# Queries as seven products of halves, and the softmax division moved behind the value products with its inverse sums passed through DRAM

## The chip, the cores and the metric

The kernel runs on one core of one Trainium2 chip, in float32 throughout. The time is device microseconds of that core; lower is better. A core has a TensorE (PE, with its weight loads shown as PEld), a VectorE (DVE), a ScalarE (ACT), a GpSimd (POOL) and a SyncE (SP), which here issues every DMA. Each engine takes its instructions in the order in which they were written.

## The reference, cut to what matters

The block is a cross-attention with adaptive layer norms: 16 batches of 1024 query rows, 64 context rows per batch, width 512, 16 heads of 32.

```python
def _ada_ln(x, c, W_ss, b_ss):
    h = (x - mean(x)) / sqrt(var(x) + EPS)
    scale, bias = split(silu(c) @ W_ss + b_ss, 2)
    return (1.0 + scale)[:, None, :] * h + bias[:, None, :]

xq  = _ada_ln(x_q,  t_vec, Wss_q,  bss_q)       # (16, 1024, 512)
xkv = _ada_ln(x_kv, t_vec, Wss_kv, bss_kv)      # (16, 64, 512)
q = xq @ Wq + bq
k, v = xkv @ Wkv + bkv                          # 16 heads of 32
attn = softmax(q @ k^T / sqrt(32))              # over the 64 context rows
out = attn @ v
return x_q + (out @ Wp + bp)
```

## The kernel before, in words

**Tiling.** The 16 x 1024 query rows are 32 blocks of 512 rows, so two blocks belong to one batch (`i // BPB`). The order of all work is written out by hand: instructions go to each engine's queue in the order of the calls, and the tile pools only add the waits. A start-up stage treats blocks 0 to 2 with separate calls, a loop `for i in range(3, NB - 2)` treats the steady state, and a written-out tail ends blocks 30 and 31. One pass of the loop works on several blocks at once: scores and softmax of block i, values and projection of block i-1, the last projection products of block i-2, queries of block i+1, and the layer norm of blocks i+2 and i+3.

**One block.** `q_stats` (VectorE, L251) and `q_scale` (a few tiny ScalarE and GpSimd operations, L265 to L274) make mean and inverse deviation. `hidden` (ScalarE, L302) normalises. `turn` (VectorE 32 x 32 transposes, L439) and `move` (16 DMAs on SP's queue, L452) bring the features onto the partitions in `xt`. The adaptive scale is folded into the weights: `query_weights` (L431) makes a scaled copy of Wq for every batch, and the shift is folded into a bias. `queries(i, o)` makes one 128-column piece of the queries by four matmuls of 128x128 weights on 512 rows (L487), and `queried` adds the bias on ScalarE (L504). `scores(i, z)` makes the logits of one half of the context with 32x32 tiles of TensorE (L515). Each half lies in two PSUM tiles; VectorE takes the maxima of a tile (L526, a reduction with a transpose inside) and ScalarE then copies it to SBUF (L533). `maxima` joins the halves and spreads them over 32 columns by a transpose (L547), `subtract` takes them away on GpSimd (L560), `weights` is the exponential (L566).

**The division.** `sums(i, z)` makes the row sums of each half (L571), `inverse` adds them, takes the reciprocal and spreads it (L547), and `divide` multiplies both halves by it on GpSimd (L591). `mix` then forms the values with 32x32 tiles (L611).

**The projection.** For blocks 2 to 28 it is already a product of halves: the 512 x 512 product is cut into quarters and made of seven products instead of eight (`product(i, n)`, L740, each 4 matmuls of 256 columns), with sums of the weights made once (`weight_sums`), sums of the value rows made per block (`mixed_halves` on ScalarE, `row_sums` on VectorE, L710 to L714, `last_row_sum` on GpSimd, L719), and each product's bank added to the residual on VectorE (`added`, L754). The accumulation runs through two PSUM banks that are never cleared between products. Two of the four quarters of a block's output need a bias, which `biased` writes into the banks ahead of the products. The other blocks use `project` (L638).

**Memory.** PSUM is two tiles of two banks for scores and values (`ps_s`) and four single banks (`ring`, in the loop 0 and 1 for queries and 2 and 3 for the projection). In SBUF the score tiles `s` rotate through four buffers, the query features `xt` and the queries `qt` through two.

A matmul of float32 shows as two records in the trace, so four matmuls are "x8".

## Time and profile before

| what | value |
|---|---|
| median of 3 runs | 1092.11 us (1091.81 to 1092.3) |
| the profiled execution, whole | 1093.58 us |
| its span, first to last instruction | 1091.8 us |
| granted TensorE clock over the span | 0.998 |
| TensorE busy | 1073.8 us (98%) |
| VectorE busy | 872.9 us (80%) |
| GpSimd busy | 673.4 us (62%) |
| ScalarE busy | 602.6 us (55%) |
| DMA, mean share of 16 engines | 41.4% |

In the tables of the profile a row is one group of instructions: line, engine, operation, output and inputs, count, then busy time and mean nanoseconds of one, then the idle time just before them and what ended it. In a timeline a row is a run of equal instructions: start in us, us from the first one's start to the last one's end, engine, line, operation, count. Matmul records overlap each other by a few tenths of a us, so the price of a run of matmuls is best read from start to start. One loop pass without context work takes 30.84 us; of every four passes one transposes a context tile (+0.43 us) and one makes keys and values (+7.2 us).

### The profile page before, as it was taken

To read this page: it belongs to the slowest core of one execution; us is meant where nothing else is said; L and a number is where in the kernel's file an instruction comes from. 1 tells how busy PE (TensorE), PEld (TensorE's weight loads), DVE (VectorE), ACT (ScalarE), POOL (GpSimd) and SP (SyncE) were. 2 spreads that over 40 slices of the span, in tenths; PEclk is the share of its full clock that TensorE was granted. 3 is DMA by queue.
4 is the path that set the end of the run, shared out by engine and by line. 5 is a ranking of instruction groups with operands and counts; after the bars stand their busy time and mean duration, and the time that the engine had idled before them with its cause. 6 is when DMAs were issued, how large, how long until landed. Compare 5 with 4: busy or idle time off the path is not lost.

```text
span 1091.8 us, 20467 instructions
## 1 busy us (share of the span) xinstructions
PE 1073.8 (98%) x8290; PEld 613.2 (56%) x8290; DVE 872.9 (80%) x1105; ACT 602.6 (55%) x895; POOL 673.4 (62%) x356
## 2 busy tenths in 40 slices
PE   6999999999999999999999999999999999999998
PEld 4534365555755557555566556555665555755533
DVE  5689678888698886989868889688887888697893
ACT  3665545656367572666736575465655656356430
POOL 0247786766748765666737766566765666748830
PEclk9999999999999999999999999999999999999999
DMA  9733532444334443444444443353442444333402
GB/s 338 241 110 116 153 116 103 145 152 149 94 111 144 142 145 113 122 127 142 138 141 128 117 140 126 131 155 121 131 143 91 145 156 136 97 111 100 137 30 87
DMA packets 80525, 145.36 MB, mean 133 GB/s; under 512 B 10504, under 2 KB 10656, under 8 KB 80432
## 3 DMA queue, kind: packets, MB, share of 16 engines
q1 hardware_dynamic: 80432, 144.07, 41.4%
q8 instruction: 65, 1.06, 0.4%
q14 instruction: 28, 0.23, 0.1%
HBM read 77.97 MB, written 33.55 MB: 102 GB/s over the span
## 4 chain that ended last, share of the span: by engine, by line
PE 92%; DMA 3%; DVE 3%; POOL 1%; SPq 1%; issue 0%; ACT 0%; DVEq 0%; POOLq 0%
PE pq L487 38%; PE pp L740 31%; PE po L611 6%; PE ps L515 6%; PE pp L638 6%; PE pv L375 2%; PE pk L347 2%; DMA wss_kv<-in_L_xcond_Wss_kv_dram 1%; DMA b_p_sb<-in_L_xcond_bp_dram 1%; POOL s L591 1%; DVE l L571 1%; DMA x<-in_x_dram 1%; SPq L452 0%; DVE vb L547 0%; DVE s L560 0%; DVE m L526 0%
## 5 line engine op out<-in xcount | busy, mean ns | idle before, releaser
L487 PE MATMUL pq<-xt,wq 128*128 128x512 f32 x1024 | 467.4, 600 | 2.2 <-DMA xt<-ht 1.1
L591 POOL TENSOR_TENSOR s<-s,vb 128x2048 f32<-128x2048 f32 x62 | 280.0, 4538 | 189.6 <-DVE vb L547 183.8
L560 POOL TENSOR_TENSOR s<-s,mb 128x2048 f32<-128x2048 f32 x58 | 262.8, 4554 | 136.7 <-DVE mb L547 136.7
L487 PEld LDWEIGHTS pq<-xt,wq 128*128 128x128 f32 x1024 | 188.8, 190 | 245.6 <-issue 240.4
L533 ACT COPY s<-ps 128x1024 f32<-128x1024 f32 x128 | 129.6, 1012 | 192.0 <-DVE m L526 184.5
L754 DVE TENSOR_TENSOR r<-pp,r 128x512 f32<-128x512 f32 x189 | 126.5, 669 | 69.9 <-PE pp L740 67.1
L504 ACT ACTIVATE qt<-pq,bqs 128x512 f32<-128x512 f32 x128 | 87.6, 685 | 153.0 <-PE pq L487 149.3
L526 DVE TRANSPOSE_TENSOR_REDUCE m<-ps 128x32 f32<-128x1024 f32 x128 | 152.2, 1227 | 24.6 <-PE ps L515 24.6
L566 ACT ACTIVATE s<-s 128x2048 f32<-128x2048 f32 x64 | 122.1, 1908 | 69.0 <-POOL s L560 63.7
L571 DVE TRANSPOSE_TENSOR_REDUCE l<-s 128x64 f32<-128x2048 f32 x64 | 146.6, 2301 | 6.5 <-ACT s L566 6.5
L740 PE MATMUL pp<-w_p_sb,ot 128*128 128x256 f32 x648 | 148.7, 379 | 0.0
L740 PEld LDWEIGHTS pp<-w_p_sb,ot 128*128 128x128 f32 x648 | 123.1, 190 | 28.3 <-ACT x L302 6.5
L740 PE MATMUL pp<-WT,ot 128*128 128x256 f32 x432 | 104.9, 386 | 0.0
L740 PE MATMUL pp<-WT,s 128*128 128x256 f32 x432 | 102.8, 381 | 0.0
L740 PEld LDWEIGHTS pp<-WT,s 128*128 128x128 f32 x432 | 81.5, 190 | 32.2 <-issue 20.8
L302 ACT ACTIVATE x<-x,rstdq 128x512 f32<-128x512 f32 x128 | 97.2, 811 | 3.9 <-POOL rstdq L274 2.2
L740 PEld LDWEIGHTS pp<-WT,ot 128*128 128x128 f32 x432 | 79.8, 190 | 32.4 <-DVE r L754 16.8
L251 DVE BATCH_NORM_STATS2 bs<-x 128x6 f32<-128x512 f32 x128 | 84.4, 660 | 3.9 <-DMA x<-in_x_dram 3.9
L439 DVE STREAM_TRANSPOSE ht<-x 128x512 f32<-128x512 f32 x124 | 77.5, 680 | 5.8 <-DMA xt<-ht 3.3
L547 DVE STREAM_TRANSPOSE mb<-m 128x2048 f32<-128x2048 f32 x32 | 74.0, 2311 | 6.7 <-POOL s L591 3.7
L515 PE MATMUL ps<-qt,kt 32*32 32x512 f32 x2048 | 76.1, 600 | 1.4 <-DVE kt L355 0.8
L547 DVE STREAM_TRANSPOSE vb<-v 128x2048 f32<-128x2048 f32 x32 | 74.0, 2311 | 3.0
(111 smaller groups left out, 871.2 us busy)
## 6 DMA issues: line engine op xcount, KB each, us to landing
x<-in_x_dram SPq DMA_DIRECT2D x32, 1024.0 KB, 5.6
r<-in_x_dram SPq DMA_DIRECT2D x32, 1024.0 KB, 5.5
xt<-ht SPq DMA_DIRECT2D x496, 64.0 KB, 2.0
out_dram<-r SPq DMA_DIRECT2D x54, 512.0 KB, 2.8
out_dram<-r SPq DMA_DIRECT2D x20, 256.0 KB, 2.0
wss_q<-in_L_xcond_Wss_q_dram SPq DMA_DIRECT2D x2, 1024.0 KB, 8.9
ctx<-in_ctx_dram SPq DMA_DIRECT2D x8, 256.0 KB, 5.5
wss_kv<-in_L_xcond_Wss_kv_dram SPq DMA_DIRECT2D x2, 1024.0 KB
```

Source lines behind the costliest of these rows:

```text
L302: nc.scalar.activation(dst, src, AF.Identity, bias=rstd[:, 1, j : j + 1], scale=rstd[:, 0, j : j + 1])
L487: nc.tensor.matmul(pq.rearrange("p (g n) -> p g n", g=4), lhsT=wq_tiles[b][:, c, o * P : (o + 1) * P], rhs=xt[:, :, c, :], start=(c == 0), ...
L515: nc.tensor.matmul(pss[r // 2][32 * c : 32 * c + 32, r % 2, :], lhsT=kt[rows, c, z * HK : (z + 1) * HK], rhs=qt[rows, c, :], start=True, s ...
L526: nc.vector.tensor_reduce(m_tiles[i][:, z, 2 * e : 2 * e + 2, :], pss[e].rearrange("p r (j a) -> p r j a", a=32), AX.X, ALU.max, apply_tra ...
L533: nc.scalar.copy(s_sb[:, 2 * e : 2 * e + 2, :], pss[e])
L547: nc.vector.transpose(t, src.unsqueeze(2).to_broadcast([P, HPC * NJ, 32]))
L560: eng.tensor_tensor(s_tiles[i, z], s_tiles[i, z], mb_tiles[i], ALU.subtract)
L566: nc.scalar.activation(p, p, AF.Exp, scale=SCALE)
L571: nc.vector.tensor_reduce(l_tiles[i][:, z], s_tiles[i, z].rearrange("p r (j a) -> p r j a", a=32), AX.X, ALU.add, apply_transpose=True,)
L591: eng.tensor_tensor(s_tiles[i, z], s_tiles[i, z], vb, ALU.mult)
L740: nc.tensor.matmul(acc[k][:, t * HO : (t + 1) * HO], lhsT=rows[:, c, t * P : (t + 1) * P], rhs=cols[:, c, :], start=new and t == 0 and c == 0,
L754: nc.vector.tensor_add(r, acc[k].rearrange("p (t h) -> p t h", t=2), r)
```

## The change

Four things change, in blocks and passes from about 4 to 29; blocks 0 to 3 and 31 keep plain queries, blocks 0 to 2 and the last two keep the old division.

1. **Queries of blocks 5 to 30** are made from halves in the manner of the projection: seven products of 4 matmuls of 256 columns. The scale and the shift are no longer folded into the weights; `scale_features` applies them to the features on ScalarE, `query_weight_sums` forms sums of the weight quarters once, `feature_sums` forms sums of the feature quarters per block on GpSimd. The results leave their two banks by ScalarE (`query_out`), by VectorE (`query_added`), and one copy from bank to bank (`query_seed`).
2. **The division of blocks 3 to 29** follows `mix`. GpSimd adds the two exponential halves (`total`), VectorE makes one row sum (`row_total`) and its reciprocal, one DMA writes the 128 x 64 inverses to DRAM and four DMAs read them back with the heads turned onto other partitions (`inverse_rows`), VectorE spreads them (`spread_rows`) and multiplies them in while it takes the values out of PSUM (`divided`).
3. **The projection's row sums** all go to GpSimd (`row_sums(i, n)`), and the seven products use another arrangement of signs, so that both biases lie in the banks and `residual_rest` is not needed.
4. **The order** of a loop pass is new: products of projection and queries alternate, layer norm runs one block further ahead, the context work is spread over three passes, in `scores(i, 0)` the copies of the two PSUM tiles are crossed, and the loop starts at block 4 behind a written-out pass for block 3. `qt` and the score tiles get fixed single buffers.

The diff, cut to its core:

```diff
+    def scale_features(i, cs=range(NC)):
+        xt, b = xt_tiles[i], i // BPB
+        for c in cs:
+            nc.scalar.activation(
+                xt[:, :, c, :],
+                xt[:, :, c, :],
+                AF.Identity,
+                scale=ss["q"][:, c, b : b + 1],
+                bias=ss["q"][:, NC + c, b : b + 1],
+            )
+    HO, HT, HC = H // 2, TB // 2, NC // 2
+    sums_of = {}
+    def query_half(m, k):
+        return w_q_sb[:, k * HC : (k + 1) * HC, m * HO : (m + 1) * HO]
+    def query_weight_sums():
+        t = qpool.tile([P, 4, HC, HO], F32, tag="wq", name="wq_sums")
+        sums_of["wq"] = t
+        tt = nc.gpsimd.tensor_tensor
+        tt(t[:, 0], query_half(1, 0), query_half(1, 1), ALU.add)
+        tt(t[:, 1], t[:, 0], query_half(0, 0), ALU.subtract)
+        tt(t[:, 2], query_half(0, 0), query_half(1, 0), ALU.subtract)
+        tt(t[:, 3], query_half(0, 1), t[:, 1], ALU.subtract)
+    def feature_half(i, k, n):
+        return xt_tiles[i][:, 2 * n : 2 * n + 2, k * HC : (k + 1) * HC, :]
+    def feature_sums(i):
+        if "xt" not in sums_of:
+            sums_of["xt"] = qpool.tile([P, 4, 2, HC, P], F32, tag="wq", name="xt_sums")
+        t = sums_of["xt"]
+        tt = nc.gpsimd.tensor_tensor
+        b12 = feature_half(i, 0, 1)
+        tt(t[:, 0], feature_half(i, 1, 1), b12, ALU.subtract)
+        tt(b12, b12, feature_half(i, 0, 0), ALU.subtract)
+        tt(t[:, 1], feature_half(i, 1, 1), b12, ALU.subtract)
+        tt(t[:, 2], feature_half(i, 1, 0), t[:, 1], ALU.subtract)
+    qa = {}
+    def query_product(i, n):
+        w, t = sums_of["wq"], sums_of["xt"]
+        a, x = {
+            1: (query_half(0, 0), feature_half(i, 0, 0)),
+            2: (query_half(0, 1), feature_half(i, 1, 0)),
+            3: (w[:, 3], feature_half(i, 1, 1)),
+            4: (query_half(1, 1), t[:, 2]),
+            5: (w[:, 0], feature_half(i, 0, 1)),
+            6: (w[:, 1], t[:, 1]),
+            7: (w[:, 2], t[:, 0]),
+        }[n]
+        k = 0 if n in (1, 6, 5, 3) else 1
+        new = n in (1, 7)
+        if new:
+            qa[k] = bank(f"pq_{i}_{n}", k)
+        for m in range(2):
+            for c in range(HC):
+                nc.tensor.matmul(
+                    qa[k][:, m * HT : (m + 1) * HT].rearrange("p (g n) -> p g n", g=2),
+                    lhsT=a[:, c, m * P : (m + 1) * P],
+                    rhs=x[:, :, c, :],
+                    start=new and m == 0 and c == 0,
+                    stop=c == HC - 1,
+                    skip_group_check=True,
+                )
+    def query_seed(i):
+        qa[1] = bank(f"pq_{i}_2", 1)
+        nc.scalar.copy(qa[1], qa[0])
+    def query_places(i, n, k, m):
+        pq = qa[k][:, m % 2 * HT : (m % 2 + 1) * HT]
+        dst = qt_tiles[i][:, m, :].rearrange("p (t g b) -> p g t b", t=NT, g=4)
+        return (
+            pq.rearrange("p (g t b) -> p g t b", g=2, t=NT),
+            dst[:, 2 * n : 2 * n + 2],
+        )
+    def query_out(i, n):
+        k, m, h = {2: (1, 0, 0), 6: (0, 1, 0), 7: (1, 1, 1), 3: (0, 0, 1)}[n]
+        if n == 2:
+            qt_tiles[i] = qpool.tile([P, NC, TB], F32, tag="qt", name=f"qt_{i}", bufs=1)
+        for o in (2 * m, 2 * m + 1):
+            src, dst = query_places(i, h, k, o)
+            nc.scalar.activation(dst, src, AF.Identity, bias=bq_t[:, o : o + 1])
+    def query_added(i, n):
+        k, h = {5: (0, 1), 4: (1, 0)}[n]
+        for o in (2, 3):
+            src, dst = query_places(i, h, k, o)
+            nc.vector.tensor_tensor(dst, src, dst, ALU.add)
...
-        for e in range(2):
+        for step in (
+            ((maximum, 0), (copied, 1), (maximum, 1), (copied, 0))
+            if crossed
+            else ((maximum, 0), (copied, 0), (maximum, 1), (copied, 1))
+        ):
+            step[0](step[1])
...
+    def total(i):
+        t = big.tile([P, HPC, TB], F32, tag=f"big{(i + 1) % 2 * 2}", name=f"sum_{i}")
+        nc.gpsimd.tensor_tensor(t, s_tiles[i, 0], s_tiles[i, 1], ALU.add)
+        sum_tiles[i] = t
+    def row_total(i):
+        lt_tiles[i] = small.tile([P, HPC, NJ], F32, tag="lt", name=f"lt_{i}")
+        nc.vector.tensor_reduce(
+            lt_tiles[i],
+            sum_tiles.pop(i).rearrange("p r (j a) -> p r j a", a=32),
+            AX.X,
+            ALU.add,
+            apply_transpose=True,
+        )
+    def inverse_rows(i):
+        lt = lt_tiles.pop(i)
+        nc.vector.reciprocal(lt, lt)
+        v = small.tile([P, NC, NJ], F32, tag="vr", name=f"vr_{i}")
+        d = dram.tile([NC, 32, HPC, NJ], F32, tag="lt", name=f"ltd_{i}")
+        nc.sync.dma_start(d.rearrange("c a r j -> (c a) r j"), lt)
+        for r in range(HPC):
+            nc.sync.dma_start(v[32 * r : 32 * r + 32], d[:, :, r, :].rearrange("c a j -> a c j"))
+        vt_rows[i] = v
+    def spread_rows(i):
+        v = vt_rows.pop(i).rearrange("p c j -> p (c j)")
+        t = qpool.tile([P, NC, TB], F32, tag="vb", name=f"vb_{i}", bufs=1)
+        nc.vector.transpose(
+            t.rearrange("p c q -> p (c q)"), v.unsqueeze(2).to_broadcast([P, NC * NJ, 32])
+        )
+        vb_tiles[i] = t
+    def divided(i):
+        vb = vb_tiles.pop(i)
+        ot_tiles[i] = opool.tile([P, NC, TB], F32, tag="ot", name=f"ot_{i}")
+        for e in range(2):
+            cs = slice(2 * e, 2 * e + 2)
+            nc.vector.tensor_tensor(ot_tiles[i][:, cs, :], po_tiles[i][e], vb[:, cs, :], ALU.mult)
...
+    def row_sums(i, n):
+        tt = nc.gpsimd.tensor_tensor
+        if n == 0:
+            s1_tiles[i] = opool.tile([P, HC, HT], F32, tag="s1", name=f"s1_{i}")
+            tt(s1_tiles[i], half_rows(i, 1, 0), half_rows(i, 0, 0), ALU.subtract)
+            tt(half_rows(i, 1, 0), half_rows(i, 1, 1), half_rows(i, 1, 0), ALU.subtract)
+        else:
+            s2_tiles[i] = opool.tile([P, HC, HT], F32, tag="s2", name=f"s2_{i}")
+            tt(s2_tiles[i], half_rows(i, 1, 1), s1_tiles[i], ALU.subtract)
+            tt(half_rows(i, 0, 1), half_rows(i, 0, 1), s2_tiles[i], ALU.subtract)
...
-    residual(2, (0, 1))
     context_features(2)
-    query_weights(2)
+    scale_features(4)
     project(1, 2)
+    load_x(6)
+    scores(3, 0, crossed=True)
+    project(1, 3)
+    ring[:] = [0, 1]
+    scores(3, 1)
+    maxima(3)
+    subtract(3)
+    queries(4, 0)
+    load_residual(3)
+    hidden(5, (0, 1))
+    biased(2, 2)
+    mix(2)
+    mixed(2)
+    hidden(5, (2, 3))
+    q_stats(6)
+    turn(5, range(NT))
+    move(5)
+    q_scale(6)
+    row_sums(2, 0)
+    load_x(7)
+    queries(4, 1)
+    product(2, 1)
+    added(2, 1)
+    product(2, 2)
+    weights(3, 0)
+    added(2, 2)
+    biased(2, 3)
+    weights(3, 1)
+    total(3)
+    queries(4, 2)
+    keys(2)
+    hidden(6, range(NT))
+    scale_features(5)
+    row_sums(2, 1)
+    turn(6, range(NT))
+    load_x(8)
+    product(2, 7)
+    q_stats(7)
+    value_products(2)
+    value_tiles(2)
+    row_total(3)
+    inverse_rows(3)
+    queries(4, 3)
+    feature_sums(5)
+    move(6)
+    q_scale(7)
...
+    for i in range(4, NB - 2):
+        a, b, n, f = i - 1, i - 2, i + 1, i + 2
         kvb = i // 4 * 2 + 2
         kv = i % 4 if kvb < B else None
         if kv == 0:
             load_context(kvb)
+        scores(i, 0, crossed=True)
+        product(b, 6)
+        added(b, 6)
+        query_product(n, 1)
+        query_seed(n)
+        added(b, 7)
         scores(i, 1)
+        product(b, 5)
+        added(b, 5)
         maxima(i)
         subtract(i)
+        product(b, 4)
+        if i + 3 < NB:
+            hidden(i + 3, (0, 1, 2))
+        query_product(n, 2)
+        query_out(n, 2)
+        product(b, 3)
+        spread_rows(a)
+        if i + 3 < NB:
+            hidden(i + 3, (3,))
+        added(b, 4)
+        added(b, 3)
+        biased(a, 2)
         load_residual(i)
+        mix(a)
+        divided(a)
+        row_sums(a, 0)
+        query_product(n, 6)
+        weights(i, 0)
+        query_out(n, 6)
         if kv == 1:
             context_hidden(kvb)
+        scale_features(f, (0, 1))
+        product(a, 1)
+        if i + 4 < NB:
+            q_stats(i + 4, (0,))
+        added(a, 1)
+        product(a, 2)
+        if i + 4 < NB:
+            q_stats(i + 4, (1,))
+        added(a, 2)
+        weights(i, 1)
+        total(i)
+        query_product(n, 7)
+        query_out(n, 7)
+        biased(a, 3)
+        scale_features(f, (2, 3))
+        row_sums(a, 1)
+        if kv == 1:
+            context_scaled(kvb)
+        if kv == 2:
+            key_products(kvb, spare(f"pk_{kvb}"))
+        if kv == 3:
+            value_products(kvb, spare(f"pv_{kvb}"))
+        if i + 3 < NB:
+            turn(i + 3, range(NT))
+        if i + 5 < NB:
+            load_x(i + 5)
+        elif i == NB - 3:
             load_residual(NB - 1)
+        query_product(n, 5)
+        query_added(n, 5)
+        if i + 4 < NB:
+            q_stats(i + 4, (2,))
+        if kv == 1:
+            context_scale(kvb)
+        if kv == 2:
+            key_tiles(kvb)
+        if kv == 3:
+            value_tiles(kvb)
+        query_product(n, 4)
+        query_added(n, 4)
+        if i + 4 < NB:
+            q_stats(i + 4, (3,), kvb=kvb if kv == 0 else None)
+        query_product(n, 3)
+        query_out(n, 3)
+        if f < NB - 1:
+            feature_sums(f)
         else:
             residual(i)
+        product(a, 7)
+        row_total(i)
+        inverse_rows(i)
+        if i + 3 < NB:
+            move(i + 3)
+        if i + 4 < NB:
+            q_scale(i + 4, kvb=kvb if kv == 0 else None)
+        if kv == 1:
+            context_shift(kvb)
...
+    scores(y, 0, crossed=True)
+    product(y - 2, 6)
+    added(y - 2, 6)
+    added(y - 2, 7)
+    scores(y, 1)
+    product(y - 2, 5)
     added(y - 2, 5)
-    scores(y, 0)
-    product(y - 2, 4)
-    added(y - 2, 4)
-    product(y - 2, 3)
-    added(y - 2, 3)
-    ring[:] = [0, 1, 2, 3]
-    load_residual(y)
-    scores(y, 1)
     maxima(y)
     subtract(y, nc.vector)
     queries(z, 0)
+    product(y - 2, 4)
+    product(y - 2, 3)
+    spread_rows(y - 1)
+    added(y - 2, 4)
+    added(y - 2, 3)
+    ring[:] = [1, 2, 3, 0]
+    load_residual(y)
     mix(y - 1)
-    mixed(y - 1)
+    divided(y - 1)
     weights(y, 0)
     queries(z, 1)
     sums(y, 0)
```

## The prediction

> **What bounds the kernel now.** I read the page's busy times and the chain that ended last first.
>
> ```profile
> PE 1073.8 (98%) x8290; PEld 613.2 (56%) x8290; DVE 872.9 (80%) x1105; ACT 602.6 (55%) x895; POOL 673.4 (62%) x356
> ...
> PE 92%; DMA 3%; DVE 3%; POOL 1%; SPq 1%; issue 0%; ACT 0%; DVEq 0%; POOLq 0%
> PE pq L487 38%; PE pp L740 31%; PE po L611 6%; PE ps L515 6%; PE pp L638 6%; PE pv L375 2%; PE pk L347 2%; DMA wss_kv<-in_L_xcond_Wss_kv_dram 1%; DMA b_p_sb<-in_L_xcond_bp_dram 1%; POOL s L591 1%; DVE l L571 1%; DMA x<-in_x_dram 1%; SPq L452 0%; DVE vb L547 0%; DVE s L560 0%; DVE m L526 0%
> ```
>
> TensorE carries 92% of the chain, and the queries (L487) are its largest line. Busy time alone would not prove this, since matmul records overlap, so I took TensorE's timeline of one plain loop pass:
>
> ```profile
> 460.60 1.14 PE L515 MATMUL ps<-qt,kt 32*32 32x512 f32 x32
> 461.67 1.99 PE L740 MATMUL pp<-WT,ot 128*128 128x256 f32 x8
> 463.50 1.89 PE L740 MATMUL pp<-w_p_sb,ot 128*128 128x256 f32 x8
> 465.32 1.14 PE L515 MATMUL ps<-qt,kt 32*32 32x512 f32 x32
> 466.39 3.70 PE L487 MATMUL pq<-xt,wq 128*128 128x512 f32 x8
> 470.02 2.35 PE L611 MATMUL po<-s,vt 32*32 32x512 f32 x64
> 472.30 3.70 PE L487 MATMUL pq<-xt,wq 128*128 128x512 f32 x8
> 475.84 3.62 PE L740 MATMUL pp<-w_p_sb,ot 128*128 128x256 f32 x16
> 479.29 3.60 PE L487 MATMUL pq<-xt,wq 128*128 128x512 f32 x8
> 482.73 1.89 PE L740 MATMUL pp<-WT,s 128*128 128x256 f32 x8
> 484.45 1.89 PE L740 MATMUL pp<-WT,ot 128*128 128x256 f32 x8
> 486.18 3.60 PE L487 MATMUL pq<-xt,wq 128*128 128x512 f32 x8
> 489.61 1.89 PE L740 MATMUL pp<-WT,s 128*128 128x256 f32 x8
> 491.43 1.14 PE L515 MATMUL ps<-qt,kt 32*32 32x512 f32 x32
> ```
>
> Start to start nothing is missing: no wait ends late, the pass is 491.43 - 460.60 = 30.83 us of matmuls. A quarter of the queries costs 3.43 us, a product of halves 1.73; either costs about 0.1 more on each side where a 32x32 stage (L515, L611) is its neighbour.
>
> Then the other engines' prices:
>
> ```profile
> L591 POOL TENSOR_TENSOR s<-s,vb 128x2048 f32<-128x2048 f32 x62 | 280.0, 4538 | 189.6 <-DVE vb L547 183.8
> ...
> L754 DVE TENSOR_TENSOR r<-pp,r 128x512 f32<-128x512 f32 x189 | 126.5, 669 | 69.9 <-PE pp L740 67.1
> ...
> L526 DVE TRANSPOSE_TENSOR_REDUCE m<-ps 128x32 f32<-128x1024 f32 x128 | 152.2, 1227 | 24.6 <-PE ps L515 24.6
> ...
> L571 DVE TRANSPOSE_TENSOR_REDUCE l<-s 128x64 f32<-128x2048 f32 x64 | 146.6, 2301 | 6.5 <-ACT s L566 6.5
> ...
> xt<-ht SPq DMA_DIRECT2D x496, 64.0 KB, 2.0
> ```
>
> Their idle times show that they wait for each other and for TensorE while TensorE waits for no one.
>
> **TensorE's part.** Four quarters with their neighbours cost 3.63 + 3.53 + 3.43 + 3.44 = 14.03 us in this pass. In the new pass stand 14 products, 14 x 1.725 = 24.15, six of them beside a 32x32 stage (+0.6), two score stages of 1.07 and one value stage of 2.28: 29.17 us instead of 30.84. That is 1.67 less, for blocks 5 to 30, so **26 x 1.67 = 43.4 us**. Weight loads grow from 32 to 56 per block at 190 ns; under a 256-column record (214 ns) the same load already hides in the projection rows, by 24 ns. The projection keeps 27 x 7 products, keys and values stay, only spread over three passes.
>
> **The other engines, per pass.** VectorE loses three row sums (0.60 start to start), one of two L571 reductions (2.28) and a small join (0.3), and gains two 128x1024 products out of PSUM (no row; between two L754 at 0.60 and L526 at 1.23 each; I take 1.15, so 2.3) and four 128x256 adds (0.36 from the 256-wide value copies, 1.44): 26.3 becomes 25.7 of 29.2. ScalarE loses 5.2 (four L504, the value copies, the scaled weights) and gains four feature scalings at 0.76, eight 256-wide copies (no row; between 0.31 for 64 columns and 0.60 for 512; 0.43) and the seed 0.5: about 21. GpSimd loses 9.06 + 1.27 + 1.27 and gains 4.53 (`total`) and eight 512-wide sums at 1.25: about 24.3. SP gains five issues at 0.6. All fit under 29.2, hidden behind TensorE; but queues are in order, so I walked one pass, t = 0 at its first score stage.
>
> - Scores 1 at 4.73; its maxima, `added` 5 and `maxima` give the spread maximum at 11.68. Subtractions end at 16.4 and 20.9, the second exponential at 22.8, `query_out` 7 at 23.7. Query product 4 needs that bank and can start at 23.95: **0.2 us of room**.
> - GpSimd: `row_sums` 0 to 23.5, `total` to 28.1; VectorE's `row_total` and reciprocal to 31.1, which is 1.9 in the next pass. Behind them wait the next maxima; their copies end at 4.2, scores 1 wants the banks at 4.73: 0.5 of room. As a loop (subtractions 9.06, row sums 2.5, total 4.53, row total 2.3, reciprocal 0.55, maxima and adds 9.2, handovers 0.5) this is 28.7 against 29.17.
> - SP: write landed at 4.0, reads issued by 6.5, landed at 8.0; `spread_rows` comes at 11.68, **3.7 of room**, and behind it are `added` 4 and 3, `divided` (its first half 0.6 ahead of product 1). The 16 moves queue behind the reads: 10.0 us of issue as now, landed at 18; `scale_features` wants them at 19.2, and behind it on ScalarE stands the second exponential: 1.2 of room.
>
> So nothing overshoots, but the rooms are tenths, and on passes with a context tile ScalarE has 0.76 more ahead of the exponential. The two passes in four that make keys or values have 3.6 us more TensorE work and absorb all of it; that leaves 14 passes. I charge 0.35 each, **4.9 us** (0 if every room holds).
>
> [...] For the two DMA hops the row is 2.0 us from issue to landing for 64 KB in 512-byte pieces. [...] I take the row: DMA is at 41%, and the 1 MB load ahead has landed by then. [...] The trace shows it once in the tail: a GpSimd add of 1.27 us took 2.79 beside a VectorE subtraction of two SBUF tiles. `divided` reads one tile from PSUM, as L754 does, beside which the 58 GpSimd subtractions stay within 4530 to 4581 ns. [...]
>
> **Once only.** The pass for block 3 does two blocks' layer norm: 16 moves end near 157, the next load of x lands near 162.6 (5.6 later), its statistics hold VectorE until 166, then value copies and the row total; the next maxima start about 3.5 us late, the scores' wait costs **3.3** (0 to 9). In the tail no query product stands between products 6 and scores 1 of block 30, which then wait **1.4** for the copies. `query_weight_sums` (4 x 1.26) fits between the end of `queries(1, 3)` at 60.6 and GpSimd's first division at 66.9; uncovered, it would delay that division, which is on the chain.
>
> **Sum.** 1091.8 - 43.4 + 4.9 + 3.3 + 1.4 = 1058.0 us of span; this execution as a whole was 1.8 above its span and 1.5 above the median of the runs, so a median of about **1058**.
>
> **Rivals.**
> - *The helper loop binds* (0.25). The 28.7 us loop over GpSimd and VectorE and ScalarE's bank release have almost no room; 7% on their prices makes the pass 30.7, 14 x 1.5 = 21.5 instead of 4.9: **1075** (1066 to 1086). For it: three of my prices have no row. Against: VectorE and GpSimd durations spread by 1%.
> - *SP's loop binds, and it gets slower* (0.09). Reciprocal, write 2.1, reads 2.4, moves 10, landing 1.4, scaling 1.6, exponential 1.9, total 4.5, row total 2.3, reciprocal and handovers 1.1: 27.3 us. If small transfers land like the worst in the table (7.4 for a move) or issue at 1.6, it grows by 4 to 6. It decides from 31.9 us (14 x 2.76 eats the 38.7 left): 4.6 more than the row. At 6 more, 14 x 4.1 + 12 x 0.6 = 65: **1117**. Against: 496 moves have a median of 2.0 and hardly vary.
> - *Seven products save nothing* (0.03). If a product costs 1.96 because its features come in two runs of 128 columns and the load's 24 ns are lost, four quarters and seven products are equal: about **1093** unless the stalls add more. Against: L487 already reads four such runs.
> - *As forecast* (0.63): 1048 to 1066.
>
> **How the numbers follow.** The runs differ by 0.05%, and about 0.2% (2.2 us) is what can be told from no change. Forecast and first rival are faster: 0.88. The third lies within with 0.02 and slower with 0.01, so slower is 0.10. The range runs from 43.4 saved and no stall (1048) into the first rival at 1080, which leaves out about 0.06 of it, the other two, and a little of the forecast.
>
> **What would show it.** Plain passes of 29.2 to 29.6 us between score stages, products of 1.73 in both groups, TensorE at 98%, small reads landing near 2 us, VectorE never idle for `v` ahead of the spread. Wrong would be: weight loads of query products waiting for ScalarE's `qt`, GpSimd subtractions over 4.6 us, ScalarE's scaling waiting for the moves' landing, or score stages waiting for copies in every plain pass.

## The result, and the profile after

The changed kernel took 1058.55 us (median of 4 runs, 1057.48 to 1060.34) against 1092.2 us for the kernel before (4 runs, 1091.81 to 1093.16). The ratio is 0.9692, with a 95% interval of 0.9675 to 0.9709: 3.1% faster. The profiled execution took 1058.86 us with a span of 1057.1 us, so the span is compared with the 1091.8 us of before: 34.7 us less.

The page of the changed kernel, its busy times, the chain that ended last and the groups that answer to those shown of before:

```profile
PE 1033.6 (98%) x8914; PEld 733.7 (69%) x8914; DVE 854.7 (81%) x1134; ACT 618.0 (58%) x951; POOL 752.7 (71%) x470
...
PE 80%; DVE 5%; POOL 5%; DMA 4%; SPq 2%; issue 2%; ACT 1%; POOLq 0%; DVEq 0%; ACTq 0%
...
L729 POOL TENSOR_TENSOR s<-s,mb 128x2048 f32<-128x2048 f32 x58 | 263.1, 4560 | 160.8 <-DVE mb L716 160.8
...
L655 ACT ACTIVATE qt<-pq,bias_t 128x256 f32<-128x256 f32 x208 | 85.8, 463 | 110.9 <-PE pq L625 110.9
...
L768 POOL TENSOR_TENSOR sum<-s,s 128x2048 f32<-128x2048 f32 x27 | 122.7, 4543 | 0.8 <-ACT s L735 0.8
...
L662 DVE TENSOR_TENSOR qt<-pq,qt 128x256 f32<-128x256 f32 x104 | 39.1, 418 | 63.1 <-PE pq L625 62.5
```

TensorE is still busy for 98% of a shorter span, and it still carries most of the chain. The other engines did not become cheaper as a whole: VectorE falls by 18 us, ScalarE rises by 15 and GpSimd by 79. GpSimd's subtraction, 4560 ns against 4554 before, kept its price. The new loop adds work to the helpers to take work from TensorE.

The timeline of TensorE over one plain pass of the changed kernel (pass 16), start in us and us from the first start to the last end:

```profile
542.48 1.14 PE L673 MATMUL ps<-qt,kt 32*32 32x512 f32 x32
543.55 2.00 PE L933 MATMUL pp<-WT,s 128*128 128x256 f32 x8
545.38 1.89 PE L625 MATMUL pq<-xt,w_q_sb 128*128 128x256 f32 x8
547.20 1.14 PE L673 MATMUL ps<-qt,kt 32*32 32x512 f32 x32
...
562.94 1.89 PE L625 MATMUL pq<-xt_sums,wq_sums 128*128 128x256 f32 x8
564.67 1.89 PE L625 MATMUL pq<-xt,wq_sums 128*128 128x256 f32 x8
...
569.85 1.89 PE L933 MATMUL pp<-WT,ot 128*128 128x256 f32 x8
571.66 0.71 PE L673 MATMUL ps<-qt,kt 32*32 32x512 f32 x16
```

The last row is cut short by the end of the view. From score stage to score stage this pass is 571.66 - 542.48 = 29.18 us. There is no wait in it, and the products of both groups stand 1.73 us apart (564.67 - 562.94). Before, the same pass was 30.83.

The small transfers, in the table of DMA issues of the changed kernel (count, size of each, median us from issue to landing):

```profile
xt<-ht SPq DMA_DIRECT2D x496, 64.0 KB, 2.0
...
vr<-ltd SPq DMA_DIRECT2D x108, 8.0 KB, 1.6
...
ltd<-lt SPq DMA_DIRECT2D x27, 32.0 KB, 1.6
```

**Where the 34.7 us are.** I compared the starts of the first score stage of every pass in the two timelines.

| stretch | after minus before, us | what it is |
|---|---|---|
| up to the scores of block 3 | -1.5 | before had a half-clock window in its start-up (granted clock 0.5 from 78.9 to 82.3 us), after had none there |
| pass 3 | -3.9 | two projection products (3.5) are put off to the tail |
| passes 4 to 29 | -35.6 | 26 x 1.67 = -43.4 (queries of blocks 5 to 30; block 4 still has plain ones), then +5.8 in pass 4 and +2.0 in all others together |
| pass 30 | +4.1 | the two products put off, and a wait of 0.6 |
| scores of block 31 to the end | +2.2 | a slower last softmax |

### The profile page after: what moved, and what is told of

The parts are those of the page before. It is cut to its first block, busy times and chain, and to the rows that moved or that the text cites. A ratio compares the mean times of both kernels' runs of the same rounds, so it can differ in the third digit from the quotient of the medians.

```text
span 1057.1 us, 22537 instructions
## 1 busy us (share of the span) xinstructions
PE 1033.6 (98%) x8914; PEld 733.7 (69%) x8914; DVE 854.7 (81%) x1134; ACT 618.0 (58%) x951; POOL 752.7 (71%) x470
## 3 DMA queue, kind: packets, MB, share of 16 engines
q8 instruction: 70, 1.15, 0.5%
## 4 chain that ended last, share of the span: by engine, by line
PE 80%; DVE 5%; POOL 5%; DMA 4%; SPq 2%; issue 2%; ACT 1%; POOLq 0%; DVEq 0%; ACTq 0%
PE pp L933 28%; PE pq L625 27%; PE po L825 6%; PE ps L673 6%; PE pp L852 5%; PE pq L542 3%; SPq L508 2%; PE pv L431 2%; PE pk L395 2%; POOL s L760 2%; DMA wss_kv<-in_L_xcond_Wss_kv_dram 2%; DMA b_p_sb<-in_L_xcond_bp_dram 1%; POOL s L729 1%; DMA x<-in_x_dram 1%; DVE s L729 1%
## 5 line engine op out<-in xcount | busy, mean ns | idle before, releaser
L729 POOL TENSOR_TENSOR s<-s,mb 128x2048 f32<-128x2048 f32 x58 | 263.1, 4560 | 160.8 <-DVE mb L716 160.8
L685 DVE TRANSPOSE_TENSOR_REDUCE m<-ps 128x32 f32<-128x1024 f32 x128 | 150.6, 1214 | 27.1 <-PE ps L673 27.1
L655 ACT ACTIVATE qt<-pq,bias_t 128x256 f32<-128x256 f32 x208 | 85.8, 463 | 110.9 <-PE pq L625 110.9
L768 POOL TENSOR_TENSOR sum<-s,s 128x2048 f32<-128x2048 f32 x27 | 122.7, 4543 | 0.8 <-ACT s L735 0.8
L933 PEld LDWEIGHTS pp<-WT,s 128*128 128x128 f32 x432 | 78.9, 192 | 54.0 <-issue 29.3
L933 PE MATMUL pp<-WT,s 128*128 128x256 f32 x432 | 109.3, 397 | 0.0
L625 PE MATMUL pq<-xt_sums,wq_sums 128*128 128x256 f32 x416 | 101.0, 386 | 0.0
L321 ACT ACTIVATE x<-x,rstdq 128x512 f32<-128x512 f32 x128 | 96.7, 807 | 4.8 <-POOL rstdq L285 3.2
L625 PE MATMUL pq<-xt,wq_sums 128*128 128x256 f32 x416 | 99.0, 381 | 0.0
L625 PEld LDWEIGHTS pq<-xt_sums,wq_sums 128*128 128x128 f32 x416 | 77.0, 190 | 31.1 <-issue 21.8
L625 PE MATMUL pq<-xt,w_q_sb 128*128 128x256 f32 x416 | 98.4, 380 | 0.1
L662 DVE TENSOR_TENSOR qt<-pq,qt 128x256 f32<-128x256 f32 x104 | 39.1, 418 | 63.1 <-PE pq L625 62.5
L565 ACT ACTIVATE xt<-xt,ss_q 128x512 f32<-128x512 f32 x112 | 84.7, 810 | 6.1 <-DMA xt<-ht 4.3
L625 PEld LDWEIGHTS pq<-xt,w_q_sb 128*128 128x128 f32 x416 | 79.1, 190 | 11.0 <-PE pp L933 0.4
```

The source lines that it names most:

```text
L321: nc.scalar.activation(dst, src, AF.Identity, bias=rstd[:, 1, j : j + 1], scale=rstd[:, 0, j : j + 1])
L565: nc.scalar.activation(xt[:, :, c, :], xt[:, :, c, :], AF.Identity, scale=ss["q"][:, c, b : b + 1], bias=ss["q"][:, NC + c, b : b + 1],)
L625: nc.tensor.matmul(qa[k][:, m * HT : (m + 1) * HT].rearrange("p (g n) -> p g n", g=2), lhsT=a[:, c, m * P : (m + 1) * P], rhs=x[:, :, c, : ...
L655: nc.scalar.activation(dst, src, AF.Identity, bias=bq_t[:, o : o + 1])
L685: nc.vector.tensor_reduce(m_tiles[i][:, z, 2 * e : 2 * e + 2, :], pss[e].rearrange("p r (j a) -> p r j a", a=32), AX.X, ALU.max, apply_tra ...
L729: eng.tensor_tensor(s_tiles[i, z], s_tiles[i, z], mb_tiles[i], ALU.subtract)
```

## The experiments

Passes are given as the time between the first score stages of one block and the next, read from TensorE's timeline. "K" is a pass with keys, "V" one with values, "T" one that turns a context tile (the last of these, pass 29, no longer has a tile to turn). Where one number stands, most passes of that kind have it; pass 4 is left out. The kernel before ran beside each group of kernels, at 1091.9 to 1092.3 us.

| kernel | median us (range) | ratio to before, 95% interval | plain | T | K | V |
|---|---|---|---|---|---|---|
| changed, again | 1057.95 (1056.88 to 1060.41) | 0.9692 [0.9679, 0.9706] | 29.2 | 29.6 | 32.8 | 33.0 |
| four quarters | 1099.08 (1098.1 to 1099.92) | 1.0062 [1.0046, 1.0079] | 30.9 | 31.3 | 34.4 | 34.7 |
| old division | 1143.78 (1142.27 to 1144.26) | 1.0469 [1.0453, 1.0485] | 32.7 | 33.4 | 35.6 | 35.4 |
| the same, deviations first | 1125.75 (1124.34 to 1127.09) | 1.0305 [1.0286, 1.0323] | 31.9 | 32.6 | 34.8 | 34.6 |
| the same, no feature sums | 1144.6 (1142.29 to 1145.86) | 1.0476 [1.0458, 1.0494] | 32.8 | 33.5 | 35.7 | 35.4 |
| no trip | 1057.73 (1056.38 to 1059.44) | 0.9684 [0.967, 0.9699] | 29.2 | 29.6 | 32.8 | 33.0 |
| two more hops | 1102.4 (1097.59 to 1103.16) | 1.0083 [1.0061, 1.0105] | 31.0 to 36.2 | 30.1 to 34.7 | 32.8 | 33.0 |
| moves first | 1117.16 (1109.94 to 1125.33) | 1.0229 [1.0175, 1.0284] | 30.9 to 33.3 | 31.5 to 33.8 | 34.2 to 35.0 | 34.8 to 37.3 |
| one more GpSimd add | 1060.2 (1058.52 to 1061.29) | 0.9704 [0.9688, 0.9721] | 29.2 | 30.0 | 32.8 | 33.0 |
| start reordered | 1055.1 (1054.05 to 1056.24) | 0.9659 [0.9646, 0.9673] | | | | |
| tail reordered | 1056.48 (1055.56 to 1056.81) | 0.967 [0.9657, 0.9684] | | | | |
| both reordered | 1052.36 (1051.78 to 1053.33) | 0.9635 [0.9622, 0.9648] | | | | |

### The changed kernel again

Run beside the three reordered kernels as their yardstick.

> The changed kernel once more, beside the three that follow: 1057 to 1060 us.

It came out at 1057.95 us. Its span is 1055.1 us where the first profile had 1057.1. Half of the difference is pass 4, 34.0 against 35.0 us, where the first execution has a half-clock window, told of below; the other half is small stalls in passes 5 to 29.

### Queries as four quarters

```diff
-        query_product(n, 1)
-        query_seed(n)
+        queries(n, 0, later=True)
...
-        query_product(n, 6)
+        queries(n, 1, later=True)
         weights(i, 0)
-        query_out(n, 6)
+        queried(n, 1)
```

The pieces 2 and 3 are undone in the same way, and `feature_sums` goes. All else, with the new order and the new division, stays.

> The changed kernel with four plain quarters of the queries (512 columns) at the places of query products 1, 6, 7 and 3; the copy from bank to bank, the adds on VectorE and the feature sums on GpSimd (5.1 us a pass) are left out, since nothing needs them. Theory (TensorE's matmuls alone are the gain): a plain pass is 30.82 us of matmuls again, 26 x 1.65 = 43 more, less some 2 us of stalls that disappear: 1098 to 1102 us, no faster than the kernel before. Rival (order, division and GpSimd row sums carry a good part of the gain): clearly under 1085 us.

It took 1099.08 us. The rest of the change without the seven products is 0.6% slower than the kernel before; the seven products alone are worth 1099.08 - 1057.95 = 41.1 us. The passes say the same: four passes in a row take 131.2 us here and 124.7 us in the changed kernel, so one pass gains 1.65 us.

### The old division in the new loop

```diff
-        total(i)
+        sums(i, 0)
...
+        sums(i, 1)
...
-        row_total(i)
-        inverse_rows(i)
+        inverse(i)
+        divide(i)
...
-        divided(a)
+        mixed(a)
```

Beyond these lines, `inverse` now also spreads the sums on VectorE, and `spread_rows` goes.

> The changed kernel with the old division from block 3 on: row sums of both halves on VectorE, inverse and spread, two multiplications on GpSimd ahead of the value products, values copied out by ScalarE; no trip through DRAM. Theory (the division is moved only to make room on GpSimd): GpSimd has 9.06 + 9.06 + 5.1 + 5.1 + 0.8 = 29.1 us of work and about 1 us of handovers in a pass of 29.18, so the 14 passes without keys or values become 30 to 31 us: 1068 to 1085 us, still faster than before. Rival (the division is worth nothing, TensorE alone decides): 1057 to 1061. Rival (the division is most of the gain): over 1085.

This expectation missed by far: 1143.78 us, slower than the kernel before, and every pass is longer, those with keys and values too. Two readings of it were open: GpSimd's load, or the order of the queues. Two more kernels asked for one each. In the first the deviations are made ahead of the division:

```diff
+        if i + 4 < NB:
+            q_scale(i + 4, kvb=kvb if kv == 0 else None)
+        if kv == 1:
+            context_shift(kvb)
         inverse(i)
         divide(i)
```

> The old division in the new loop again (1143.8 us before), with the six small GpSimd operations of the layer norm's deviations (q_scale, and context_shift) emitted ahead of inverse and divide instead of behind them. If the queue order made that kernel slow (hidden and the score copies on ScalarE waiting for deviations that sit behind 9 us of division): 1065 to 1095 us. If GpSimd's own load did (subtraction 9.05, division 9.0, row sums 5.1, feature sums 5.1, small ones 0.8: 29.1 us, and some 3 us of waiting for VectorE's inverse between them): the order changes nothing, 1136 to 1146 us.

In the second the four feature sums are left out of every pass of the loop, 5.1 us of GpSimd, so the query products read the sums of block 5:

```diff
-        if f < NB - 1:
-            feature_sums(f)
-        else:
+        if f >= NB - 1:
             residual(i)
```

> The old division in the new loop again, with the four feature sums (4 x 1.27 us on GpSimd) left out of every pass of the loop, so that query products 4, 6 and 7 read the sums of block 5 (leaves out part of the computation). If GpSimd's load made that kernel slow: its loop falls from about 33 to about 28 us, below TensorE's 29.2, and the time to 1055 to 1080 us. If the order of queues did: 1130 to 1146 us, as with the sums.

Without feature sums the time is 1144.6 us: GpSimd's load is not the cause, against what I had come to think. With the deviations first it is 1125.75 us: this one change of the queue order is worth 18.0 of the 86 us. The wait that this takes away stands in ScalarE's timeline of the first of the three kernels:

```profile
529.05 2.23 ACT L321 ACTIVATE x<-x,rstdq 128x512 f32<-128x512 f32 x3 [3.26 <-POOL rstdq L285]
```

`hidden` (L321) waits 3.26 us for deviations whose four tiny GpSimd operations are queued behind 9.0 us of division, and the value copies wait behind `hidden`. What is left is in the timelines of TensorE and VectorE of the kernel with deviations first, in a plain pass (in it L673 is the scores, L757 the spread of the inverse sums, L685 the maxima, L740 the row reduction of one half):

```profile
577.82 1.26 PE L673 MATMUL ps<-qt,kt 32*32 32x512 f32 x32
...
584.11 1.18 PE L673 MATMUL ps<-qt,kt 32*32 32x512 f32 x32 [1.38 <-ACT s L694]
...
606.06 1.99 PE L625 MATMUL pq<-xt,wq_sums 128*128 128x256 f32 x8 [0.83 <-DVE qt L662]
...
579.57 2.31 DVE L757 STREAM_TRANSPOSE vb<-v 128x2048 f32<-128x2048 f32 x1
581.81 2.34 DVE L685 TRANSPOSE_TENSOR_REDUCE m<-ps 128x32 f32<-128x1024 f32 x2
...
600.70 2.30 DVE L740 TRANSPOSE_TENSOR_REDUCE l<-s 128x64 f32<-128x2048 f32 x1
...
605.29 0.71 DVE L662 TENSOR_TENSOR qt<-pq,qt 128x256 f32<-128x256 f32 x2
```

The 2.31 us spread of the inverse sums stands on VectorE straight ahead of the next maxima, so the second scores come 6.29 us after the first instead of 4.72. One of the two row reductions stands ahead of the addition that frees the bank of a query product. Both are places that the new division leaves free: it has one reduction, and its spread comes later, behind the next maximum. In this kernel TensorE's waits for the score copies add up to 43.1 us and those for the additions to 7.9. A further 9 us lie in pass 4, which lasts 42.7 us instead of 34.0 and holds two half-clock windows; three more stand elsewhere. These causes are read from the trace; no run took them away one by one, and no run has an order made for the old division, so the 86 us are what it costs in this order and not what it must cost.

### The trip through DRAM left out

The five transfers are left out; the spread reads the inverse sums where they lie, with the heads on the wrong partitions, so this leaves out the turn of the inverse sums.

```diff
-        nc.sync.dma_start(d.rearrange("c a r j -> (c a) r j"), lt)
-        for r in range(HPC):
-            nc.sync.dma_start(v[32 * r : 32 * r + 32], d[:, :, r, :].rearrange("c a j -> a c j"))
-        vt_rows[i] = v
+        vt_rows[i] = lt
```

> The changed kernel without the five transfers: the inverse sums are spread from where they lie, so the heads get each other's inverses and the output is not the reference's; nothing else is left out. Theory (the trip is hidden with 4.8 us of room ahead of the spread): no plain pass gets shorter, 1056 to 1060 us. Rival (the trip costs time in every pass): 5 us or more faster than the changed kernel.

1057.73 us: the same as with the trip, and so are the passes. The five transfers cost nothing where they stand.

### Two more hops

```diff
-        nc.sync.dma_start(d.rearrange("c a r j -> (c a) r j"), lt)
+        nc.sync.dma_start(d0.rearrange("c a r j -> (c a) r j"), lt)
+        nc.sync.dma_start(d1, d0)
+        nc.sync.dma_start(d, d1)
```

> The changed kernel with two more transfers of the 32 KB from DRAM to DRAM between the write and the four reads, each waiting for the one before: the trip grows by some 3.7 us. Theory (what stands behind the trip is short of room, not the spread): the inverses still land near 10.2 us into the pass, ahead of the spread at 11.3, but the 16 moves land near 21 instead of 17.4, scale_features wanted them at 18.7, and the second exponential and query product 4 come 1.5 to 2.2 us late in 14 passes: 1078 to 1090 us. Rival (only the spread's wait counts): 1057 to 1061. Rival (the helpers have more room than walked): under 1066.

1102.4 us: 44 us more than the changed kernel, 12 past what I expected at most. The timelines of SP, ScalarE and GpSimd show the chain (this pass makes values), and the rows of waits (us in total, times, longest) what it does in the whole execution:

```profile
535.28 0.49 SPq L791 DMA_DIRECT2D lt<-lt  x1
537.43 0.49 SPq L792 DMA_DIRECT2D ltd<-lt  x1
539.42 1.76 SPq L794 DMA_DIRECT2D vr<-ltd  x4
541.28 11.11 SPq L508 DMA_DIRECT2D xt<-ht  x16
...
553.97 1.52 ACT L565 ACTIVATE xt<-xt,ss_q 128x512 f32<-128x512 f32 x2 [4.53 <-DMA xt<-ht]
555.39 1.90 ACT L735 ACTIVATE s<-s 128x2048 f32<-128x2048 f32 x1
...
557.36 4.53 POOL L768 TENSOR_TENSOR sum<-s,s 128x2048 f32<-128x2048 f32 x1 [3.65 <-ACT s L735]
...
ACT xt L565 <- DMA xt<-ht: 81.6, 27, 4.9
...
PE pq L625 <- ACT qt L655: 26.7, 14, 3.7
```

The four reads are issued 5.4 to 7.5 us after the write, 6.1 on average (here 7.5; the write, not shown, stands at 531.93), where the changed kernel has 1.5 to 3.5 and an average of 2.1. So the trip is 4.0 us longer, about what I expected. The moves (L508) start that much later, `scale_features` (L565) waits for them in every pass, the second exponential stands behind it, and GpSimd's `total` and the copy that frees the bank for query product 4 stand behind that. It is at product 4 that TensorE waits: in all 13 shorter passes and in pass 4, never in those with keys or values. This is the handover for which the prediction had 0.2 us of room. The loop is the one that my slower rival had summed to 27.3 us; with 4.0 us more it is 31.3. The runs agree in both respects: passes of 32.8 and 33.0 are untouched, and of the 13 shorter ones the eight without half clock last 31.1 us on average. The other five last 34.5. They contain six half-clock windows, each up to 1.7 us dear (half of 3.41 us, an estimate), where the changed kernel has none in the loop behind pass 4. Without these the 13 passes would have cost some 13 x 1.65 = 21 us, within what I expected; what I had not reckoned with is that such waits, of 1.92 to 3.75 us in these five passes, were followed by half clock.

### The moves ahead of the trip

```diff
-        inverse_rows(i)
         if i + 3 < NB:
             move(i + 3)
+        inverse_rows(i)
```

> The changed kernel with the 16 moves of the turned tile issued on SP ahead of the inverse sums' write and four reads instead of behind them. The inverse sums then land some 10 us later, about 17 us into the pass, where spread_rows takes them up at 11.3: if that wait reaches TensorE through divided and product 1, over two passes the chain from scores to scores is about 63 us instead of 58.4, 2.5 us in each of 14 passes: 1075 to 1100 us. If the order on SP is free: 1056 to 1060 us.

1117.16 us, over my range. The waits of this kernel (us in total, times, longest):

```profile
DVE vb L795 <- DMA vr<-ltd: 69.1, 25, 3.3
...
PE pp L933 <- DVE ot L805: 44.2, 25, 2.3
```

The spread waits 2.8 us in each of 25 passes, and TensorE 1.8 of it. I had expected that passes with keys and values absorb this, as they absorb the hops. They do not (34.2 and more instead of 32.8), because here TensorE waits at product 1, in the middle of the pass and ahead of the keys, whereas the hops reach it at query product 4, behind them. 25 x 1.8 = 45 us, and seven half-clock windows add up to 12 at most. So the place of the five transfers ahead of the 16 moves, which put 10 us on SP's queue, is part of what the change is worth.

### One more addition on GpSimd

```diff
+        nc.gpsimd.tensor_tensor(t[:, 0], s_tiles[i, 0][:, 0], s_tiles[i, 1][:, 0], ALU.add)
         nc.gpsimd.tensor_tensor(t, s_tiles[i, 0], s_tiles[i, 1], ALU.add)
```

> The changed kernel with one more GpSimd addition of 128x512 (1.27 us) straight before each pass's total, in all 27 passes. If the loop over GpSimd and VectorE had 0.5 us of room, 0.8 us of it is seen in each of the 14 passes without keys or values: 1058 + 11 = 1064 to 1072 us. If there is more room than 1.3 us: 1056 to 1060 us, the changed kernel's time.

1060.2 us, 2.2 more than the changed kernel run before; the intervals of the ratios overlap, so the passes decide. VectorE's timeline at the end of pass 16, first of the changed kernel, then of this one (L773 and L774 are the row total):

```profile
570.50 0.18 DVE L261 BATCH_NORM_AGGREGATE mvq<-bs 128x2 f32<-128x6 f32 x1
570.60 2.28 DVE L773 TRANSPOSE_TENSOR_REDUCE lt<-sum 128x64 f32<-128x2048 f32 x1
```

```profile
568.82 2.31 DVE L774 TRANSPOSE_TENSOR_REDUCE lt<-sum 128x64 f32<-128x2048 f32 x1 [0.91 <-POOL sum L769]
```

In the changed kernel the row total does not wait for `total` here; it is reached when VectorE is through with the statistics. Of the 1.27 us added, 0.91 show as a wait of VectorE, and 0.3 reach TensorE (second scores after 5.03 us instead of 4.72), in one pass out of four only: 6 x 0.33 = 2.0 us. The long passes with keys and values let the loop catch up. Only pass 30, behind two passes without such work and with no query product between its score stages, pays all of it, 27.67 us instead of 26.35.

### The start and the tail reordered

In the written-out pass for block 3, the next load of x goes ahead of the 16 moves, and its statistics ahead of the next turn:

```diff
     turn(5, range(NT))
+    load_x(7)
     move(5)
...
-    load_x(7)
...
+    q_stats(7)
     turn(6, range(NT))
     load_x(8)
     product(2, 7)
-    q_stats(7)
```

> The changed kernel with the load of x for block 7 issued ahead of the 16 moves of block 5, and its row statistics ahead of the transposes of block 6. Theory (the pass of block 4 loses 5.8 us because SP issues that load behind the moves, VectorE sits waiting for it, and the score stage's wait of 2.9 us then halves the granted TensorE clock for 3.4 us): 4 to 6 us faster than the changed kernel, pass of block 4 at 29.2 to 30.5 us and no half clock there. Rival (VectorE's work in that pass is too much whatever the order): under 1.5 us.

1055.1 us, 2.85 less than the changed kernel, short of what I expected. TensorE's timeline of pass 4, first in the changed kernel, then in this one:

```profile
161.96 1.98 PE L673 MATMUL ps<-qt,kt 32*32 32x512 f32 x32
163.87 2.00 PE L933 MATMUL pp<-WT,s 128*128 128x256 f32 x8
165.94 1.97 PE L625 MATMUL pq<-xt,w_q_sb 128*128 128x256 f32 x8
170.84 1.25 PE L673 MATMUL ps<-qt,kt 32*32 32x512 f32 x32 [2.94 <-ACT s L694]
172.02 3.56 PE L933 MATMUL pp<-WT,s 128*128 128x256 f32 x8
```

```profile
161.40 1.05 PE L673 MATMUL ps<-qt,kt 32*32 32x512 f32 x6
163.23 1.13 PE L673 MATMUL ps<-qt,kt 32*32 32x512 f32 x26 [0.77 <-ACT qt L560]
...
167.94 1.14 PE L673 MATMUL ps<-qt,kt 32*32 32x512 f32 x32
```

The wait of 2.94 us is gone. The pass still takes 31.81 us, 2.6 more than a plain one. Most of what remains is the first score stage, which waits for the copy of the query quarter straight before it; that wait was not touched.

In the tail, the residual of block 30 gets its bias behind the division instead of ahead of it, both on GpSimd:

```diff
     weights(y, 1)
-    residual(y)
...
     inverse(y)
     divide(y)
+    residual(y)
```

> The changed kernel with the bias add of block 30's residual put behind its division on GpSimd. Theory (that add waits 17 us for its load, so the division runs late and beside VectorE's subtraction of block 31, both with two SBUF inputs, and that subtraction took 7.7 us instead of 4.5): 1.5 to 3 us faster than the changed kernel. Rival (the overlap costs nothing on the last chain, or the add then collides in the same way): within 1 us.

1056.48 us, 1.5 less. The intervals of the ratios overlap, so the trace decides again: from the first scores of block 31 to the end it takes 53.4 us, as the kernel before did, instead of the changed kernel's 55.6 and 55.7. The timelines of GpSimd, VectorE and TensorE in the tail, first in the changed kernel, then in this one:

```profile
1003.16 4.96 POOL L332 TENSOR_TENSOR r<-r,b_p_sb 128x512 f32<-128x512 f32 x4 [17.20 <-DMA r<-in_x_dram]
1008.07 8.99 POOL L760 TENSOR_TENSOR s<-s,vb 128x2048 f32<-128x2048 f32 x2
...
1013.70 7.72 DVE L729 TENSOR_TENSOR s<-s,mb 128x2048 f32<-128x2048 f32 x2
...
1017.12 1.15 PE L825 MATMUL po<-s,vt 32*32 32x512 f32 x32 [0.90 <-POOL s L760]
```

```profile
1004.03 9.00 POOL L760 TENSOR_TENSOR s<-s,vb 128x2048 f32<-128x2048 f32 x2 [17.82 <-DVE vb L716]
1012.99 9.09 POOL L332 TENSOR_TENSOR r<-r,b_p_sb 128x512 f32<-128x512 f32 x4
...
1013.90 5.80 DVE L729 TENSOR_TENSOR s<-s,mb 128x2048 f32<-128x2048 f32 x2
...
1015.34 2.35 PE L825 MATMUL po<-s,vt 32*32 32x512 f32 x64
```

The division no longer waits for the bias additions and no longer runs beside VectorE's last subtraction. That pair of subtractions falls from 7.72 to 5.80 us; in the kernel before it took 4.47. It now has the bias additions beside it, and these pay as well: 9.09 us for four instead of 4.96, of which two take 3.34 each.

Both edits together:

> Both of these edits together: the sum of their gains, 1050 to 1053 us.

1052.36 us, 5.6 us less than the changed kernel, where the two gains add up to 4.3, and a ratio of 0.9635 to the kernel before. This is the fastest version.

## Why the prediction was right

The median asked for was about 1058 us and 1058.55 came out. The terms, one by one:

- **Prices without a row**: 0.36 us start to start for the 256-wide copies (0.43 taken), 0.34 for the 256-wide additions (0.36), 1.13 to 1.14 for `divided` (1.15): right, the copies a little dear.
- **TensorE's part**, 26 x 1.67 = 43.4: right. Plain passes are 29.18 us against 29.17 in the sum. The T pass (29.6) is 0.44 longer because it carries four transposes, which stood in another of the four passes before.
- **The stalls in 14 passes**, 4.9: too high. Passes 5 to 29 hold about 2 us of stall, in the second execution under 1. In the plain passes nearly every handover of the walk was met in time; I charged 0.35 a pass because the rooms were tenths. GpSimd's loop had about 0.95 us of room (1.27 added, 0.3 seen) where I had 0.5.
- **The pass behind block 3**, 3.3 (0 to 9): the mechanism is shown by the reordered start, the size was low. The second scores wait 2.94 us as forecast; the first scores wait too, for their own queries, which the sum did not have. The pass is 4.8 us over a plain one in the second execution, and 5.8 in the first, which has a half-clock window there.
- **The tail**, 1.4: low. Passes 30 and 31 together with the two products put off cost 2.4 more. The wait of scores 1 of block 30 is about 0.6. The missing term is the last softmax: division on GpSimd beside a subtraction on VectorE.
- **Not in the sum**: 1.5 us that before lost to a half-clock window in its start-up. The forecast's span of 1058.0 met 1057.1 because the stalls were 3 too dear, the pass behind block 3 and the tail 3.5 too cheap, and this window was missed. That the number is so close is luck in part, since errors of 3 and 3.5 us cancelled; that TensorE's own 43.4 us carry the gain is not.

**The trip.** I took the row of 2.0 us for the two hops and it was even less, 1.6 for each, issued in 0.4 instead of 0.6: `vr` lands about 6.5 us into the pass instead of 8.0. What a dearer trip costs is shown by the kernel with two more hops: its trip is 4.0 us longer, and it loses 44 us, of which 1.65 in each of the 13 shorter passes came without half clock.

**GpSimd beside VectorE.** In the loop the row was right: GpSimd's subtraction stays at 4560 ns beside `divided`, whose other operand is in PSUM. In the tail both engines had two inputs in SBUF, and there it was VectorE that paid (7.72 against 4.47 us for the two subtractions), which I had not charged.

**The rivals.** The helper loop does not bind: 1.27 us more on it cost 2 us, not 11. Seven products do save, 41.1 us by the kernel that undoes them. SP's loop was the best of the three: it does not bind, but its sum (31.3 us with 4.0 added, 31.1 seen), its nearly untouched long passes and its turning point (4.6 us more than the row) are near what the kernel with two more hops showed; with half clock on top, that kernel is 0.8% slower than the one before.

**What the prediction did not see** is how much the new division matters. It counted as a rearrangement that saves VectorE and GpSimd time. In the new loop the old division costs 86 us more. A run shows 18.0 of it to be queue order and rules out the feature sums' load on GpSimd; that most of the rest is queue order too is read from the trace.

## What to carry to other kernels

Where one engine has no gaps, sum its own instructions from start to start, then walk one pass over every other queue and write down the room at each handover: the first sum gives the gain, the rooms tell which small additions are free. A room of half a microsecond was enough here, since longer passes in between let a late loop catch up; but a delay that reached the bounding engine ahead of the longer work was not absorbed. Here the division was worth what it left free in the queues, not its own duration, and this was only seen when it was put back into the new order.

## What the runs showed of the hardware

**Half clock.** In the trace the granted clock falls to 0.5 for stretches of 3.413 us, or about twice that (in the kernel with two more hops, two query products in a row from 458.5 us take 3.75 and 3.19 us, where 1.97 and 1.89 are usual). In the changed kernel one such stretch runs from 171.8 to 175.2 us: the eight records of one product at 172.02 take 3.56 us, where such a run takes 2.00 elsewhere. In the 3.41 us before it TensorE was without a matmul for 2.45. The next one starts at 1055.9 us, behind the last matmul; the two starts lie 259 times 3413.3 ns apart. In the kernel before, those at 78.9 us and at 1092.6 (behind the end of the span) lie 297 times 3413.3 ns apart.

The profiles of the 14 kernels, divided into windows of that length in step with these stretches, from 150 to 1010 us, show what stood ahead of half clock. All 24 windows at full clock with more than 2.0 us without a matmul (2.12 and up) were followed by half clock; of the 3487 with less, three were (1.75, 1.92 and 1.99 us), and 1.98 us is the most that was not. The second execution of the changed kernel has the same wait of 2.94 us and no half clock (mean clock 1.0); there the edge of a window divides the wait, and the fuller window holds 1.98. The start-up differs: in the kernel before, a window with 0.97 there was followed by half clock.

Executions of the changed kernel with a mean clock of 1.0, 0.998 and 0.997 have spans of 1055.7, 1057.1 and 1058.5 us, so half clock goes along with most of its spread. In the kernels with two more hops and with the moves first, seven half-clock windows each (mean clock 0.989) make up to 12 us.

**Two engines on SBUF.** In the tail of the changed kernel the first of VectorE's two subtractions took 5.52 us and the second 2.28. The first starts at 1013.70, GpSimd's division ends at 1017.06: 3.4 us beside it, in which next to nothing was done, since the 2.2 us that follow are the price of a whole subtraction. The division kept its 4.52 us per half. It goes the other way too. In the kernel with the tail reordered, two of GpSimd's additions took 3.34 us instead of 1.27, and each ended 1.14 us after the subtraction beside it. The second subtraction took 3.37 us and ended 2.15 us after the addition beside it. So in these records the two engines went in turn: whichever was first ran to its end, and the other did its work after it. In all of them VectorE's instruction had two inputs in SBUF; in the loop, beside `divided` with one input in PSUM, GpSimd's subtraction stayed at 4560 ns.

**Small transfers.** 8 KB and 32 KB transfers landed 1.6 us after their issue (median; 3.2 at most) and held SP's queue for 0.4 and 0.3 us each, while the 64 KB moves took 2.0 and 0.6.
